# A hand-written order for TensorE: how long scan matmuls are held back for matmuls of the same array shape

## Chip, core and metric

The kernel runs on one core of a Trainium2 chip. The metric is the device time of one execution in microseconds (us). Before the change the median of three runs is 8417.75 us (8404.57 to 8426.19).

## What is computed

An image tensor `x` of shape (4, 96, 64, 64), so 4096 positions in each of 4 batches, goes through four residual layers:

```
x = x + L0(gn(x))        # 3x3 convolutions, a deformable convolution, and a selective scan in 4 directions
x = x + L1(gn(x))        # 3x3 convolution to 384 channels, gate, layer norm, 3x3 convolution back
t = tokens(x)
t = t + L2_attn(ln(t)); t = t + L2_ffn(ln(t))   # FFT over the 4096 tokens and back; a small quantized MLP
t = t + L3_attn(ln(t)); t = t + L3_ffn(ln(t))   # linear attention; the same kind of MLP
```

The part that sets the pace is the selective scan of L0, for 4 batches, 4 directions `k`, 192 channels and 16 states, over 4096 positions:

```
h = h * exp(dt * A) + (dt * u) * B      # per channel and state, position after position
y = sum over the 16 states of h * C
```

## The kernel before

**The scan.** It runs over batches, directions and four pieces of 1024 positions (`STEP`), 64 visits in all. One visit has 24 steps (`scan`, L1095 to L1179): 16 states for the first 128 channels, and 8 steps in which two states of the other 64 channels share the 128 partitions. So there are 64 x 24 = 1536 steps. Each does the following:

- SP loads one row of C, broadcast over the partitions (L1118 to L1126, tile `cb`, 3 buffers);
- PE broadcasts one row of B into the PSUM tile `pb` (L1127 to L1135, 2 buffers), with bf16 matmuls whose weights are 64x64 (four of them) or 64x128 (two of them);
- DVE multiplies `pb` by `dt*u` (L1136), ACT makes `hs = exp(dt*A)` (L1138, 5 buffers), DVE runs the scan over `hs` and `pb` (L1140), ACT copies the carry;
- POOL (in a few steps DVE) multiplies `hs` by `cb` (L1145);
- PE sums over the states by adding `hs` into the PSUM tile `yp` (L1146 to L1156), with f32 matmuls whose weights are 64x64 (four of them, `ident`) or 128x64 (two of them, `fold`).

**The fillers.** Everything else (the phases n, s, a, c, p, d and e: convolutions, norms, FFT, MLPs) is called the fillers here. Their matmuls are mostly of shape 128x128 in the array and write into only two PSUM tiles (`ps`, L600) as long as the scan runs. Once the scans are over, the tiles `pb` and one `yp` serve as further filler banks (L568 to L570).

**The order.** No scheduler of the framework orders the work. `Orders` records every operation, and `order()` (L303 to L492) plays the program through with estimated costs (`way`, `LATENCY`), always giving an engine the operation of the lowest rank among those whose inputs are ready at that time. The outcome is one fixed instruction stream for each engine, written out by `give()` (L498 and L504; so nearly every instruction in the profile has the line L504). A rank is the number of the scan step that the operation belongs to. `spread` (L1511) gives PE's fillers 300 added to their share of the steps (`LEAD`, L1577), so that a scan matmul goes ahead of nearly every filler that is ready too. The kernel's program is the same data flow whatever order comes out.

**The patience rule.** `part()` (L175) rounds the rows and columns of a matmul's weights up to 32, 64 or 128: this is its shape in the array. In the choice for PE (L387 to L396), the picked operation is put back if its shape differs from that of the matmul ordered last, no other ready operation has its shape, and fewer than `PATIENCE` nanoseconds have passed since its inputs were ready. The ready operation of the lowest rank that keeps the present shape goes first:

```
            if e == PE and ops[pick[1]].part != part and t < ops[pick[1]].ready + PATIENCE:
                if not any(ops[x[1]].part == ops[pick[1]].part for x in able[e]):
                    near = [x for x in able[e] if ops[x[1]].part == part]
```

The planner charges `CHANGE` = 95 ns for each change of shape.

**Zero matmuls.** Where PE would stand idle for more than 480 ns in the plan, and the columns streamed in the last 3413 ns are fewer than `WARM`, the planner inserts bf16 matmuls of zeros (L444 to L447, written out at L498; in the profile `yp<-nothing`). [...] `counted()` (L169) says how much a matmul counts for `WARM` and `ENOUGH`: its columns, four times for f32, in proportion to its rows, and by half for at most 64 weight columns.

**The end.** The fillers `phase_p`, `phase_d` and `phase_e` of the last batch need its scans, so they follow after them (L1563 to L1566), with more room and more banks.

Of the kernel before, what the change touches and what calls it, by code (L numbers as in the profile page):

```python
# [83 lines left out]

CHANGE = 95.0

PATIENCE = 1200.0

WARM, ZEROS = 8000, 512
PAGE = 2048  # L90
# [3 lines left out]
def columns(ap):  # L94
    n = 1
    for s in ap.shape[1:]:
        n *= s
    return n
# [6 lines left out]
class Orders:  # L105
# [63 lines left out]
    def counted(self, kwargs):  # L169

        k, m = kwargs["lhsT"].shape
        n = columns(kwargs["rhs"]) * (4 if kwargs["rhs"].dtype == F32 else 1)
        return n * k / 128 * (0.5 if m <= 64 else 1)

    def part(self, kwargs):  # L175

# [126 lines left out]
    def order(self):  # L303
# [58 lines left out]
        while ordered < len(ops):  # L362
# [15 lines left out]
            if e == ACT and ops[pick[1]].table not in (0, table):  # L378

                near = [x for x in able[e] if ops[x[1]].table in (0, table) and x[0] < pick[0] + 4]  # L380
                if near:
# [4 lines left out]
                    pick = other  # L386
            if e == PE and ops[pick[1]].part != part and t < ops[pick[1]].ready + PATIENCE:  # L387

# [1342 lines left out]
```

## Time and profile before

| | before |
|---|---|
| median of 3 runs | 8417.75 us |
| the profiled execution | 8409.08 us, its span 8407.3 us |
| first and last `pb` multiplication of the scan | 339.1 us and 7367.3 us after the start |
| matmul records on PE, zeros among them | 32888, 3672 |
| zero matmuls in the program | 3978 |
| mean granted TensorE clock | 0.95 |
| f32 matmul records, scan sums (`ident`) | 8192 for the program's 4096 |

Three things are needed to read it. First, an f32 matmul shows as two records in the profile, as the last row says. Second, matmuls overlap, so a record's own duration (some 0.6 us for 512 f32 columns) is not what it costs PE in a stream; the distance from one start to the next is. Third, "idle before, releaser" is the time that an engine stood idle in front of an instruction, with what ended it. Since each engine has a fixed stream, an instruction that isn't ready holds up everything behind it on its engine.

The profile falls into three stretches: a head until about 340 us without scans, the scans until about 7378 us, and a tail of 1029 us with fillers alone.

### The profile page before, as it was taken

To read this page: it belongs to the slowest core of one execution; us is meant where nothing else is said; L and a number is where in the kernel's file an instruction comes from. 1 tells how busy PE (TensorE), PEld (TensorE's weight loads), DVE (VectorE), ACT (ScalarE), POOL (GpSimd) and SP (SyncE) were. 2 spreads that over 40 slices of the span, in tenths; PEclk is the share of its full clock that TensorE was granted. 3 is DMA by queue.
4 is the path that set the end of the run, shared out by engine and by line. 5 is a ranking of instruction groups with operands and counts; after the bars stand their busy time and mean duration, and the time that the engine had idled before them with its cause. 6 is when DMAs were issued, how large, how long until landed. Compare 5 with 4: busy or idle time off the path is not lost. (4 is left out here: it accounts for less than half of the span.)

```text
span 8407.3 us, 101328 instructions
## 1 busy us (share of the span) xinstructions
PE 7487.2 (89%) x32888; PEld 2586.1 (31%) x33196; DVE 6557.9 (78%) x4658; ACT 4460.7 (53%) x7020; POOL 5317.5 (63%) x3147
## 2 busy tenths in 40 slices
PE   7898888989889998889989899978998899999989
PEld 2322222222222223232222222233322232244354
DVE  1398897777899999979898899986789999942324
ACT  3456644465646645555566666435465666423325
POOL 1278997865676668876776667685677667621202
PEclk8998999999999999999999999989999999999988
DMA  7688879899877788997678876889977866874442
GB/s 198 174 228 233 244 197 252 231 226 217 226 209 204 185 232 241 260 255 219 193 186 216 209 205 194 236 216 263 234 196 191 202 198 197 236 212 133 112 158 69
DMA packets 1247110, 1742.37 MB, mean 207 GB/s; under 512 B 607086, under 2 KB 683059, under 8 KB 1243636
## 3 DMA queue, kind: packets, MB, share of 16 engines
q1 hardware_dynamic: 1246580, 1735.87, 76.7%
q8 instruction: 263, 4.31, 0.2%
q14 instruction: 267, 2.19, 0.1%
HBM read 1473.58 MB, written 261.81 MB: 206 GB/s over the span
## 5 line engine op out<-in xcount | busy, mean ns | idle before, releaser
L504 POOL TENSOR_TENSOR arena<-arena 128x1024 f32<-128x1024 f32 (+3 forms) x2568 | 5012.4, 1974 | 2193.6 <-ACT arena L504 1150.7
L504 DVE TENSOR_TENSOR_SCAN arena<-arena,pb 128x1024 f32<-128x1024 f32 x1536 | 3573.7, 2329 | 288.3 <-ACT arena L504 173.7
L504 PE MATMUL ps<-arena 128*96 128x512 f32 (+10 forms) x8158 | 2774.4, 554 | 59.1 <-ACT arena L504 24.0
L504 ACT ACTIVATE arena<-arena,nega 128x1024 f32<-128x1024 f32 x1536 | 1754.8, 1149 | 1377.6 <-PE yp L504 1242.4
L504 DVE TENSOR_TENSOR pb<-pb,arena 128x1024 f32<-128x1024 f32 x1536 | 1860.7, 1213 | 338.6 <-PE pb L504 242.9
L504 PEld LDWEIGHTS ps<-arena 128*96 128x96 f32 (+6 forms) x8158 | 1028.5, 168 | 1463.7 <-issue 1219.8
L504 PE MATMUL yp<-arena,ident 64*64 64x512 f32 x8192 | 1137.7, 625 | 167.3 <-POOL arena L504 162.9
L498 PE MATMUL yp<-nothing 128*128 128x512 bf16 x3672 | 1005.0, 399 | 31.7 <-issue 24.4
L504 PE MATMUL pb<-arena,selb 64*64 64x512 bf16 x5120 | 626.8, 397 | 265.3 <-DVE arena L504 260.4
L504 PE MATMUL yp<-arena,fold 128*64 128x512 f32 x2048 | 579.4, 651 | 144.8 <-POOL arena L504 139.8
L504 ACT COPY arena<-arena 128x1 f32<-128x1 f32 x1536 | 283.4, 187 | 776.7 <-DVE arena L504 771.7
L504 ACT COPY arena<-ps 96x512 f32<-96x512 f32 (+6 forms) x636 | 332.8, 530 | 551.2 <-PE ps L504 494.2
L504 DVE TENSOR_TENSOR arena<-arena 96x512 f32<-96x512 f32 (+5 forms) x250 | 341.5, 1374 | 337.1 <-DMA arena<-rsd 135.9
L498 PEld LDWEIGHTS <-nothing 128*128 128x128 bf16 x3978 | 357.6, 101 | 767.0 <-issue 495.3
L504 ACT ACT_TABLE_LOAD x429 | 550.4, 1283 | 64.5 <-PE yp L504 53.5
L504 PEld LDWEIGHTS <-selb 64*64 64x64 bf16 x5120 | 202.0, 103 | 1089.1 <-issue 1084.1
L504 POOL TENSOR_TENSOR arena<-arena,half 128x4 f32<-128x4 f32 (+1 forms) x240 | 249.2, 1042 | 420.3 <-DMA arena<-vard 327.9
L504 PEld LDWEIGHTS yp<-arena,ident 64*64 64x64 f32 x8192 | 231.9, 133 | 793.2 <-POOL arena L504 405.1
L504 ACT CAST arena<-ps 128x512 bf16<-128x512 f32 (+2 forms) x542 | 305.4, 593 | 125.3 <-PE ps L504 117.3
L504 DVE BATCH_NORM_STATS2 arena<-arena 96x6 f32<-96x512 f32 (+1 forms) x192 | 130.4, 682 | 290.1 <-ACT arena L504 208.2
L504 PE MATMUL pb<-arena 64*128 64x192 f32 (+7 forms) x1104 | 304.3, 431 | 23.1 <-issue 9.6
L504 ACT ACTIVATE arena<-arena 96x512 f32<-96x512 f32 (+3 forms) x445 | 256.3, 591 | 116.3 <-DVE arena L504 109.5
(178 smaller groups left out, 4579.4 us busy)
## 6 DMA issues: line engine op xcount, KB each, us to landing
arena<-cr_d SPq DMA_DIRECT2D x1024, 512.0 KB
arena<-cr_d SPq DMA_DIRECT2D x1024, 256.0 KB
arena<-wmd SPq DMA_DIRECT2D x128, 576.0 KB
y_d<-arena SPq DMA_DIRECT2D x384, 128.0 KB
arena<-u_d SPq DMA_DIRECT2D x64, 512.0 KB
arena<-u_d SPq DMA_DIRECT2D x128, 256.0 KB
arena<-y_d SPq DMA_DIRECT2D x256, 128.0 KB
arena<-rsd SPq DMA_DIRECT2D x160, 192.0 KB
```

The costliest lines, as they stand in the source:

```text
L498: self.nc.tensor.matmul(i, start=alone, stop=alone, skip_group_check=True, **self.zeros)
L504: getattr(getattr(self.nc, NAMES[op.engine]), call)(*args, **kwargs)
```

## The change

`PATIENCE` goes from 1200 to 300, so a matmul that would change PE's array shape is held back for at most 300 ns of planned time. Besides, `counted()` counts a matmul with at most 32 weight columns as a quarter of its columns, where it was a half:

```diff
-PATIENCE = 1200.0
+PATIENCE = 300.0
...
-        return n * k / 128 * (0.5 if m <= 64 else 1)
+        return n * k / 128 * (0.25 if m <= 32 else 0.5 if m <= 64 else 1)
```

Nothing else is edited. The planner then writes out another order for every engine and, for the operations that may run on several engines, partly another engine.

## Prediction

> **What bounds the kernel now.** I read the page first, then three stretches, then who waited for whom, then DVE's largest groups, then a few microseconds of PE in order of time. Busy shares alone:
>
> ```profile
> PE 7487.2 (89%) x32888; PEld 2586.1 (31%) x33196; DVE 6557.9 (78%) x4658; ACT 4460.7 (53%) x7020; POOL 5317.5 (63%) x3147
> ```
>
> No engine is full over the whole span. Split at the first and last scan step (columns: span, then busy time and instructions of PE, PEld, DVE, ACT, POOL, granted clock, DMA share, GB/s):
>
> ```profile
> core 0: us, PE busy (x) PEld busy (x) DVE busy (x) ACT busy (x) POOL busy (x), PEclk, DMA share, GB/s
> 340.00:7378.00 7038.00, 6275.47 (x28280) 2020.51 (x28551) 6166.31 (x4001) 3968.40 (x6188) 5099.27 (x2893) 0.96 0.82 219
> 7378.00:8407.00 1029.00, 943.63 (x3607) 460.90 (x3630) 354.90 (x587) 363.14 (x624) 188.39 (x178) 0.93 0.47 137
> ```
>
> While scans run, DVE is 88% busy (6166 of 7038 us) and PE 89%, of which 841 us are zero matmuls (the same view for `nothing` alone). DVE idles 872 us. In the tail DVE is a third busy and PE 92%: the tail is PE's. The chain that ended last, complete only for the last 348 us, agrees: 25% of 1029 us, some 258 us of it, is PE. DVE's two scan instructions:
>
> ```profile
> L504 DVE TENSOR_TENSOR_SCAN arena<-arena,pb 128x1024 f32<-128x1024 f32 x1536 | 3573.7, 2329 | 288.3 <-ACT arena L504 173.7 <-DVE pb L504 4.1
> L504 DVE TENSOR_TENSOR pb<-pb,arena 128x1024 f32<-128x1024 f32 x1536 | 1860.7, 1213 | 338.6 <-PE pb L504 242.9 <-POOL arena L504 93.0 <-issue 1.2
> ```
>
> A step costs DVE 1213 + 2329 = 3542 ns, 1536 steps 5441 us: the floor of the scan stretch. PE makes DVE stall in two ways: directly, when the broadcast of B is late (243 us), and through ACT, whose exp needs an `hs` buffer that the sum over states has yet to read (part of 174 us). The waits, in us, times, longest:
>
> ```profile
> ACT arena L504 <- PE yp L504: 1345.6, 832, 11.2
> POOL arena L504 <- DMA arena<-cr_d: 610.2, 284, 8.0
> PE yp L504 <- POOL arena L504: 302.8, 270, 11.9
> PE pb L504 <- DVE arena L504: 270.2, 268, 10.7
> DVE pb L504 <- PE pb L504: 242.9, 199, 6.5
> ```
>
> So the coupling has two directions: DVE waits for PE 199 times, 1.22 us on average, and PE waits for DVE and POOL 573 us. And this is what a hold looks like (start, length, last the number of records):
>
> ```profile
> 2998.90 2.82 PE L504 MATMUL ps<-arena 128*96 128x512 f32 x6
> 3001.64 1.09 PE L504 MATMUL yp<-arena,ident 64*64 64x512 f32 x8
> 3002.67 0.39 PE L504 MATMUL pb<-arena,selb 64*128 64x512 bf16 x2
> 3002.89 1.02 PE L504 MATMUL ps<-arena 64*96 64x512 f32 x2
> 3003.84 1.09 PE L504 MATMUL yp<-arena,ident 64*64 64x512 f32 x8
> ```
>
> Runs of convolution matmuls stand between the scan's pieces. The weight loads of the run at 3005 us start every 0.43 us (3006.12, 3006.55, 3006.98), so a record costs 0.43 us and an f32 matmul, which is two, 0.86. Two records take 3003.84 - 3002.89 = 0.95 us up to the next shape, 0.09 more than 2 x 0.43. I take **0.09 us for a change of shape**.
>
> [...] PE stands 270 us before `pb` matmuls while fillers are queued behind them. [...] I use counts times distances for PE, not its 89%.
>
> **The change part by part.** The two programs' instruction orders can be compared without running; no time is in them, only counts.
>
> 1. *Shorter hold.* 300 ns is less than one 0.86 us filler, 1200 ns is up to two. A scan matmul that is ready while fillers of one shape run is let in about 0.9 us earlier. Taken stall by stall in the trace, with at most 0.9 us off each, DVE's waits for `pb` could lose 137 us and its waits for exp 70 us: **207 us** is the upper bound. Only stalls with a held choice gain; others come from a filler already running or from several sums in a row. The order gives a second measure. Before the last state sum stand 5550 filler matmuls now, and 5490 after the change; at the ends of batches 1, 2, 3 and 4 the lag is 72, 144, 78 and 60. Fillers go through at 5550/7378 us = 0.752 per us. If that rate stays, the scans end 60/0.752 = **80 us** earlier. I take 80, under half the bound; the other end is nothing, or a loss (rival 1).
>
> 2. *More changes of shape.* 4774 become 5132: 358 x 0.09 = 32 us of PE, 317 of them (29 us) before the last sum. They lie beside DVE's floor as long as PE has slack in zeros (841 us), and the 80 us contain them, since fillers squeezed by them lag. Without that cover they cost 29 us.
>
> 3. *Left-over fillers.* Sixty matmuls move past the scans into the tail: 34 convolutions, 6 centrings and 16 norm sums of 512 f32 columns (56 x 0.86 = 48 us) and 4 small ones. With 41 more changes (4 us) it is 52 us if PE is full there; by matmuls (60 of 1700 in 1029 us) it is 36. DVE's 23 more elementwise operations in the tail fall into its idle two thirds. I take **45**. The early tail is where they land, so they delay the last batch's own chain.
>
> 4. *The new count for narrow weights.* It lowers what single-column matmuls (norm sums) count for the clock, so it can only ask for more zeros. Yet zeros go from 3978 to 3957. At 3.34 us for 15 in the chain of waits, 0.22 each, that is 5 us less, in idle time anyway. I take 0; the bound is a few us each way.
>
> 5. *Other engines.* ACT's table loads go from 429 to 435, 6 x 1283 ns = 8 us, on an engine busy 53%: hidden. DVE takes over 7 wide products from POOL (7 x 2.4 = 17 us, from the 30 such groups it had) and gives up about as much else during the scans: 0. SP's queue of loads is reordered along with its readers; the order shows the same 7902 DMAs. A `cb` load that is behind another one now is in POOL's 610 us, and can become rival 2.
>
> The sum against the profiled execution's own 8409.08 us: -80 + 45 = -35, 8374. It is 8.7 us under the median of the runs, and the difference carries over: 8417.75 - 35 = **8383 us**.
>
> **Rivals.** (1) *PE's throughput is the limit, and it ends slower.* Then the scans end no earlier. PE's work over the whole program goes up by 32 us of changes less 5 us of zeros, so 8445; and because the stream is fixed, scan matmuls put earlier hold up the fillers behind them whenever DVE or POOL is later than planned: if PE's 573 us of such waits grow by a tenth, 8500. It decides as soon as the scans gain less than the 45 us that the tail costs. For it: PE's matmuls between two broadcasts, counted in the order at 0.86 us for 512 f32 columns, 0.22 for bf16, small shapes side by side once, 0.09 a change, come to 3.8 us on average with the zeros, more than DVE's 3.54; 60 left-over matmuls are hardly more than what the changes displace. Against it: 841 us of zeros are no work, and DVE does stall for `pb`. (2) *Another wait takes over.* DMA moves 219 GB/s at a share of 0.82 in the scans, and POOL waits 610 us for `cb`. If DVE's gain turns into waits of POOL for rows of C, the gain shrinks to about the tail's cost: 8418. For it: in some slices of the page DMA is at 9 tenths. Against: those waits are 284 of 1536 steps. (3) *All stalls in reach go*: -207 + 52 = -155, 8263. Against it: PE's longest runs between two broadcasts hardly get shorter in the order (238 stretches of over 5 us of PE's work become 220). (4) That the change does nothing is excluded: runs of 128x128 fillers rise from 1393 to 1611.
>
> **How the numbers follow.** Forecast (scans win 60 to 130 us, 8335 to 8392) 0.43; rival 3 and what lies towards it 0.13; rival 2 and small gains (8392 to 8443) 0.18; rival 1 0.26. About 0.3% (25 us) is what a measurement of this kernel can tell from no change. Faster is the first two, 0.56; within 0.3% 0.18; slower 0.26. The range leaves out a tenth on each side: from 8275, short of rival 3, to 8465, which takes in rival 1 without much blocking. The forecast's own range is 8335 to 8392.
>
> **What would show it.** Right: the last `pb` multiplication starts near 7290 us rather than 7367; DVE's wait for `pb` falls from 243 us towards 160; the tail grows from 1029 to about 1075. Wrong: the last multiplication comes no earlier (rival 1), PE's waits for DVE and POOL grow beyond 573 us (blocking), or POOL's wait for `cr_d` grows by as much as DVE's falls (rival 2). A tail that doesn't grow would make step 3 too dear.

## The result, and the profile after

The changed kernel takes 8480.94 us (median of four runs, 8462.86 to 8497.82); before stood at 8411.16 us beside it. The ratio is 1.0077, with a 95% interval of 1.0051 to 1.0103: slower, where 0.4% faster was forecast, and above the range. The profiled execution takes 8462.86 us, the fastest of the four and 53.8 us more than the one of before (8409.08 us). PE is TensorE, DVE VectorE, ACT ScalarE, POOL GpSimd, and SP SyncE, which issues the loads and stores.

First the stretches, split where the scans of this kernel begin and end (columns as before: span, busy time of PE, PEld, DVE, ACT, POOL, clock, DMA share, GB/s):

```profile
328.00:7353.00 7025.00, 6330.94 (x28408) 1978.30 (x28407) 6183.79 (x3996) 3962.33 (x6169) 5075.83 (x2869) 0.95 0.82 218
7353.00:8461.00 1108.00, 1021.46 (x3773) 481.18 (x3772) 365.22 (x610) 378.12 (x651) 192.54 (x182) 0.93 0.47 134
```

The scans are over a little earlier, but the tail has grown from 1029 to 1108 us, and PE is as full in it as before (92%, a tenth of the tail with zeros both times). The waits (total, times, longest):

```profile
ACT arena L504 <- PE yp L504: 1431.5, 893, 16.8
POOL arena L504 <- DMA arena<-cr_d: 613.2, 252, 11.9
PE yp L504 <- POOL arena L504: 259.3, 260, 8.2
PE pb L504 <- DVE arena L504: 213.6, 234, 6.1
DVE pb L504 <- PE pb L504: 176.8, 151, 7.2
```

DVE's wait for the broadcast of B fell from 242.9 to 176.8 us, as forecast. The two waits of PE for DVE and POOL did not grow but fell, from 573 to 473 us, and POOL's wait for rows of C stayed (610 and 613 us). DVE's two scan groups:

```profile
L504 DVE TENSOR_TENSOR_SCAN arena<-arena,pb 128x1024 f32<-128x1024 f32 x1536 | 3573.4, 2329 | 318.8 <-ACT arena L504 208.5 <-DVE pb L504 2.3
L504 DVE TENSOR_TENSOR pb<-pb,arena 128x1024 f32<-128x1024 f32 x1536 | 1859.8, 1212 | 274.4 <-PE pb L504 176.8 <-POOL arena L504 93.0 <-DMA arena<-f2p 1.9
```

The same work, 64 us less idle before the multiplication, but 30 us more before the scan (288.3 then): DVE's wait for ACT's exp, which was to shrink, grew from 173.7 to 208.5 us. And ACT waited longer for `yp`, 1431.5 us after 1345.6. So of what the earlier broadcasts saved, half was lost again at the exp. In the stretch of the scans DVE's idle time fell from 872 to 841 us, its work grew from 6166 to 6184 us, and the stretch begins 12 us earlier (328 after 340): -31 + 18 - 12 = -25 us at its end, and no more.

Where the time went is told by the last batch's fillers. The stores that end its phases, first in the kernel before, then after (the two starts are the first and the last of the kernel, and the last is the last batch's):

```profile
L504 SPq DMA_DIRECT2D x2p<-arena x32: 314/370/1321, 2242.4 to 7506.9; - x32
...
L504 SPq DMA_DIRECT2D x1d<-arena x32: 303/365/551, 2428.8 to 7616.8; - x32
...
L504 SPq DMA_DIRECT2D q_d<-arena x32: 303/319/1285, 3822.9 to 8338.1; - x32
```

```profile
L504 SPq DMA_DIRECT2D x2p<-arena x32: 303/368/709, 2335.3 to 7536.9; - x32
...
L504 SPq DMA_DIRECT2D x1d<-arena x32: 304/371/545, 2498.6 to 7657.1; - x32
...
L504 SPq DMA_DIRECT2D q_d<-arena x32: 303/320/574, 3990.1 to 8390.3; - x32
```

The last scan ends at 7371 us before and at 7347 after, 24 us earlier. Yet the first half of `phase_p` (`x2p`) ends 30 us later, its second half (`x1d`) 40, and the stores of queries 52. Counted from the last state sum, the first `x2p` row comes after 10 us before and after 68 us now. The same holds for the other batches: at their ends the scans stand 58, 40 and 51 us earlier than before, and the fillers' stores of `x2d` 97, 84 and 55 us later. The edit did give the scans PE's time, and the fillers, which end last, lost more than the scans won.

What stands at the head of the tail in the chain of waits of the changed kernel (start, length, what; some of its longest pieces):

```profile
7359.18 10.47 PE ps L504 x24
7371.54 12.36 PE pb L504 x28
7393.09 6.23 PE pb L504 x16
7415.71 4.94 POOL arena L504 x4
7421.53 4.79 DMA arena<-y_d
7430.32 5.50 DMA rsd<-arena
7436.80 4.75 DMA arena<-rsd
```

First some 30 us of left-over convolutions (until 7382 us), and only then the norm of the last `phase_p`, a chain of small DMAs. PE sums its first mean (weights `over`, 128*128) 34 us after the last state sum; in the kernel before this stood 39 us ahead of the last state sum.

### The profile page after: what moved, and what is told of

Read it like the earlier page. It is cut to its first block, busy times and chain, and to the rows that moved or that the text cites. A ratio compares the mean times of both kernels' runs of the same rounds, so it can differ in the third digit from the quotient of the medians.

```text
span 8461.1 us, 101588 instructions
## 1 busy us (share of the span) xinstructions
PE 7607.5 (90%) x33175; PEld 2559.4 (30%) x33175; DVE 6585.2 (78%) x4675; ACT 4468.6 (53%) x7029; POOL 5298.5 (63%) x3127
## 5 line engine op out<-in xcount | busy, mean ns | idle before, releaser
L504 DVE TENSOR_TENSOR_SCAN arena<-arena,pb 128x1024 f32<-128x1024 f32 x1536 | 3573.4, 2329 | 318.8 <-ACT arena L504 208.5
L504 DVE TENSOR_TENSOR pb<-pb,arena 128x1024 f32<-128x1024 f32 x1536 | 1859.8, 1212 | 274.4 <-PE pb L504 176.8
L504 PEld LDWEIGHTS ps<-arena 128*96 128x96 f32 (+7 forms) x8022 | 991.7, 168 | 1512.6 <-issue 1230.7
L498 PE MATMUL yp<-nothing 128*128 128x512 bf16 x3957 | 1069.0, 398 | 1.2 <-DVE half L504 1.2
L504 ACT ACT_TABLE_LOAD x435 | 558.1, 1283 | 76.4 <-PE yp L504 68.5
L504 PE MATMUL pb<-arena 64*128 64x192 f32 (+8 forms) x1080 | 302.7, 437 | 28.5 <-DMA arena<-f2p 9.1
L504 POOL MEMSET arena<- 96x16 f32 (+3 forms) x302 | 49.5, 179 | 427.6 <-PE ps L504 179.3
```

The lines of the kernel that those rows point to most:

```text
L498: self.nc.tensor.matmul(i, start=alone, stop=alone, skip_group_check=True, **self.zeros)
L504: getattr(getattr(self.nc, NAMES[op.engine]), call)(*args, **kwargs)
```

## The experiments

All times are ratios to the kernel before on the same chip. Theories: A, the fillers' use of PE ends the kernel, and changes of shape and interrupted runs cost it; B, the new count is the cause; C or L, it is the luck of the one order that came out.

**The change taken apart, a larger dose, and a neighbour.**

```diff
-PATIENCE = 1200.0
+PATIENCE = 300.0       # p300_alone
+PATIENCE = 2400.0      # p2400
+PATIENCE = 1190.0      # p1190_null
...
-        return n * k / 128 * (0.5 if m <= 64 else 1)
+        return n * k / 128 * (0.25 if m <= 32 else 0.5 if m <= 64 else 1)   # count_alone, PATIENCE 1200
```

> PATIENCE 300 with the old count of narrow weights. Theory A (more array-shape changes and interrupted fillers slow the chain of fillers that ends last): the order has 5100 changes against 4774, so the loss comes with it: +40 to +70 us, scans ending 20 to 60 us earlier and the tail longer by 60 or more. Rival B (the count is the cause): within 20 us of before. Rival C (which order comes out is luck): any time between -60 and +80, without a tie to the number of changes.

> PATIENCE 1200 with the new count. Its order has 4762 changes (12 fewer than before) and 4143 zero matmuls (165 more). Theory A: within 25 us of before. Rival B (the count is the cause): +40 to +70. Rival C (luck): anything from -60 to +80.

> PATIENCE 2400, the dose in the other direction, old count. 4539 changes (235 fewer), and 5684 fillers before the last sum (134 more). Theory A: faster, -20 to -60 us: scans end later than 7371 us, the tail is shorter than 1030 us by more. The forecast's own reasoning (late scan matmuls stall the vector engine): slower by 20 to 100, its wait for pb grows beyond 243 us. Rival C (luck): either.

> PATIENCE 1190, a change of under one percent of the wait: it changes some choice early on, after which the order differs everywhere, with 4760 changes against 4774. Theory A: within 15 us of before. Rival C (luck of the order): it shows the scatter that any other order brings; over 25 us either way would say that +54 to +70 us is not far outside it.

Measured: `p300_alone` 1.0004 (0.9993 to 1.0014), `count_alone` 1.0067 (1.0053 to 1.0081), `p2400` 1.0063 (1.0046 to 1.008), `p1190_null` 1.0041 (1.0027 to 1.0056). Theory A as put there missed all four: the shorter wait alone costs nothing here (its scans end at 7373 us, no earlier, and its tail is only 8 us longer), the count alone costs 56 us, the longer wait isn't faster, and 1190 isn't within 15 us. Rival B met the two runs that it spoke of, and the forecast's own reasoning met `p2400`: slower by 53 us, with a longer wait for `pb`. But a wait of 1190 instead of 1200, which means nothing, costs more than half of what the change costs. So one order for each setting can't tell a cause. At the far end of the dose, what moves is where the time lies. In `p2400`:

```profile
344.00:7506.00 7162.00, 6364.67 (x28968) 2072.26 (x28968) 6235.59 (x4032) 4021.67 (x6249) 5118.50 (x2913) 0.95 0.82 217
7506.00:8496.00 990.00, 893.78 (x3317) 431.29 (x3314) 314.77 (x537) 349.80 (x603) 169.59 (x159) 0.92 0.46 130
```

```profile
DVE pb L504 <- PE pb L504: 294.5, 182, 11.3
```

A longer wait gives the longest wait for `pb`, the latest scans and the shortest tail of all orders here: the reverse of the changed kernel.

**More neighbours, to see the scatter.** Only `PATIENCE` differs, with the old or the new count:

```diff
-PATIENCE = 1200.0
+PATIENCE = 1210.0      # p1210_null; with the new count c1210_null
+PATIENCE = 310.0       # p310_null; with the new count a310_null
+PATIENCE = 1190.0      # with the new count c1190_null
+PATIENCE = 290.0       # with the new count a290_null
```

> PATIENCE 1210, old count: a second neighbour of before, whose order differs from it as a matter of chance. If the order of before is a lucky one (theory L), slower by 0.2 to 0.7%, as PATIENCE 1190 was by 0.41%. If 1190 was the odd one, within 0.2%.

> PATIENCE 310, old count: a neighbour of PATIENCE 300 with the old count, which stood at 1.0004. Theory L (any other order costs 0 to 0.8%, patience does nothing on average): anywhere from 1.000 to 1.008. Theory P (a shorter wait helps by about 0.4% against neighbours of 1200): below 1.002 again.

> PATIENCE 310 with the new count: a neighbour of the changed kernel. Theory B (the new count costs some 0.6%, patience nothing): 1.006 to 1.009. Theory L (luck of the order): 1.000 to 1.008, where a time near 1.002 would show that the changed kernel's loss is no property of its two edits.

> PATIENCE 1190 with the new count: a neighbour of the run with the count alone, which stood at 1.0067. Theory B: 1.005 to 1.009. Theory L: 1.000 to 1.008. Its order has 4167 zero matmuls, 189 more than before; if zeros were what costs, it would be the slowest of the four.

> PATIENCE 1210 with the new count, a third neighbour of the run with the count alone (1.0067, 1.0044 so far). Theory B (the new count costs some 0.4% on average): 1.003 to 1.007. Theory L (only luck of the order, scatter 0.4%): anything from 0.995 to 1.008. It has 3896 zero matmuls, 82 fewer than before, where the two others had 165 and 189 more.

> PATIENCE 290 with the new count, a third neighbour of the changed kernel (1.0077, 1.0015 so far). Theory B: 1.003 to 1.008. Theory L: 0.995 to 1.008. Whatever the time, the shorter wait should show as before: the vector engine's wait for pb under 190 us, the scans done before 7371 us after the start, a tail over 1044 us.

Measured: `p1210_null` 0.9955 (0.9938 to 0.9972), `p310_null` 1.0035 (1.0024 to 1.0046), `a310_null` 1.0015 (1.0003 to 1.0028), `c1190_null` 1.0044 (1.0028 to 1.0061), `c1210_null` 1.0037 (1.0023 to 1.0051), `a290_null` 1.0005 (0.9993 to 1.0016). 1190 and 1210 lie 0.86% apart with before between them: theory L holds for any single setting, and `p1210_null` is faster than both kernels, where a lucky order of before would have had it slower. Theory P is out (1.0035), and theory B missed both neighbours of the changed kernel and `c1190_null` (1.0044, just below) and met `c1210_null`. The wait for `pb` of `a290_null` is 125 us and its tail 1065, as put there, but its scans end at 7378 us and not before 7371. Zero matmuls don't explain it: with the new count, 3896 of them (`c1210_null`) and 4167 (`c1190_null`) give nearly the same time.

**The price of a change of shape, with the order held.** Between two 128x128 matmuls that follow each other without a pause in the plan, at every fourth such place where a sum is open, one matmul of zeros with one column is added to the open sum; `extra_flat` adds it in the shape 128x128, so without a change:

```diff
+                if part == whole == op.part and opened is not None and t - free[PE] < 1:
+                    self.met += 1
+                    if self.met % 4 == 0:
+                        out.append((t, (opened, flip)))
...
+                self.nc.tensor.matmul(i[0][:64, :1], start=False, stop=False, skip_group_check=True, **self.one)
+    nc.one = {"lhsT": nothing[:64, :64], "rhs": nothing[:64, 128:129]}    # extra_flat: all 128 rows and columns
```

> The order of before, unaltered, with 765 added one-column matmuls of zeros of shape 64x64, each between two 128x128 matmuls that follow each other: 1530 more changes of shape, some four times the 358 of the change, and nothing else moves. Theory A (PE's time is what ends the kernel, a change costs 0.09 us): 1530 x 0.09 = 138 us and more, 1.016 or above. Slack theory (changes lie beside the vector engine's floor): under 40 us, below 1.005. A fourth of what is measured over the next run is what the change's own 358 cost.

> The same 765 added matmuls at the same places, of shape 128x128, so without any change of shape: the control. 765 x 0.03 to 0.1 = 25 to 75 us of PE if PE is the limit, within 20 us of before if there is slack.

Measured: 1.0171 (1.0155 to 1.0187) and 1.0050 (1.0033 to 1.0066). The added ones, and DVE's wait in the same kernel `extra_changes` (there the line that writes out the order is L513):

```profile
L503 PE MATMUL yp<-nothing x765: 187/188/212, 88.2 to 8570.6; 64*64 64x1 bf16 x192
```

```profile
DVE pb L513 <- PE pb L513: 270.3, 244, 5.2
```

One added matmul and the convolution behind it, in `extra_changes` and then in `extra_flat`:

```profile
3019.29 0.19 PE L503 MATMUL yp<-nothing 64*64 64x1 bf16 x1
3019.41 1.96 PE L513 MATMUL ps<-arena 128*96 128x512 f32 x4
```

```profile
3032.76 0.17 PE L503 MATMUL yp<-nothing 128*128 128x1 bf16 x1
3032.79 1.08 PE L513 MATMUL ps<-arena 128*96 128x512 f32 x2
```

Between two convolution records of this form (128*96, 512 columns) the distance from start to start is 430 ns in the median, 456 with the flat matmul between them and 639 with the other (159 places each). So a change of shape costs PE (639 - 456)/2 = 92 ns, as the forecast had it. At the end of the kernel, the difference of 1.21% of 8438 us (before beside them) is 102 us for 1530 changes, or 83 to 121 us by the two intervals: 0.067 us each, three quarters (0.6 to 0.9) of what they cost on PE. Taken together, added matmuls and changes cost PE 765 x 209 ns = 160 us, and 144 us (1.71%) arrive, nine tenths. DVE's wait for `pb` hardly moves (243 to 270 us) while the kernel grows by 143 us (medians), so DVE's floor hides little: by far the most of an added PE time reaches the end. Theory A is met, the slack theory is out. The change's 358 changes of shape thus cost some 24 us (19 to 28), 0.28%. Here the order is the same in all three kernels, and no luck is in it.

**Is it the count, or the order?**

```diff
-PATIENCE = 1200.0
+PATIENCE = 1180.0      # p1180_null
+PATIENCE = 1220.0      # p1220_null; with the new count c1220_null
+PATIENCE = 290.0       # p290_null
+PATIENCE = 320.0       # with the new count a320_null
+PATIENCE = 280.0       # with the new count a280_null
```

> PATIENCE 1180, old count. If the new count costs some 0.35% (theory B): 0.996 to 1.004, and below 1.002 on average with the next two. If there is only luck: 0.995 to 1.008, on average near 1.003.

> PATIENCE 1220, old count: the same two expectations as for 1180. It also tells whether 1210 at 0.9955 has a region of good orders about it (below 0.998) or stands alone.

> PATIENCE 290, old count: the same two expectations as for 1180. By the price of a change of shape alone (337 more than before, 0.067 us each: 23 us) 1.0027. The wait for pb under 190 us and a tail over 1044 us.

> PATIENCE 1220, new count: its order is the same as that of PATIENCE 1210 with the new count (1.0037) up to the third batch. Theory B: 1.002 to 1.007. Only luck: 0.995 to 1.008.

> PATIENCE 320 with the new count: a neighbour of the changed kernel, 298 more changes of shape than before. By the measured price of a change (0.067 us) alone 1.0024; with a cost of the new count of 0.4% on top 1.006; only luck 0.996 to 1.008. The vector engine's wait for pb under 190 us.

> PATIENCE 280 with the new count: a neighbour of the changed kernel, 361 more changes of shape than before. By the price of a change alone 1.0029; with the new count 1.007; only luck 0.996 to 1.008. The vector engine's wait for pb under 190 us.

Measured: `p1180_null` 0.9996 (0.9987 to 1.0004), `p1220_null` 1.0010 (1.0 to 1.0019), `p290_null` 1.0023 (1.0013 to 1.0033), `c1220_null` 1.0101 (1.0087 to 1.0115), `a320_null` 0.9973 (0.9963 to 0.9984), `a280_null` 1.0062 (1.0039 to 1.0086). In groups of neighbours (means; the last scan's end from the start, the tail from there, from one profile each):

| wait, count | kernels | ratio, mean and range | DVE's wait for `pb`, us | DVE's scans' wait for exp, us | last scan ends, us | tail, us |
|---|---|---|---|---|---|---|
| 1180 to 1220, old | 5 | 1.0000 (0.9955 to 1.0041) | 216 | 181 | 7404 | 1030 |
| 290 to 310, old | 3 | 1.0021 (1.0004 to 1.0035) | 167 | 205 | 7368 | 1082 |
| 1190 to 1220, new | 4 | 1.0062 (1.0037 to 1.0101) | 192 | 182 | 7453 | 1037 |
| 280 to 320, new | 5 | 1.0026 (0.9973 to 1.0077) | 154 | 214 | 7363 | 1080 |

The waits for `pb` are under 190 us in `p290_null`, `a320_null` and `a280_null`, as put there. The times fit no single theory: the three new orders with the old count average 1.0010, as theory B asks, but `c1220_null` lies above what either theory allows, and `a320_null` is faster than before, where B asks for 1.006. `c1210_null` and `c1220_null`, whose orders are the same up to the third batch, differ by 0.64%.

Three things stand out. On average the shorter wait takes a fifth to a quarter off DVE's wait for `pb`, adds 24 to 32 us to its wait for exp, ends the scans earlier and makes the tail 43 to 52 us longer, with either count. What it does to the time isn't told apart from the scatter: with the old count it costs 0.2% on average, about what the price of the shapes asks (0.28%), with the new count it gains 0.36%, and both are within two standard errors of nothing. And the changed kernel, at 1.0077, is the slowest of its five neighbours, whose mean is 1.0026: going by this mean, more than half of its loss (0.51 of 0.77%) belongs to the order that came out.

Whether the new count costs by itself stays open. Nine orders with it average 1.0042, eight without it 1.0008; with a scatter of 0.4% and 0.3% that is two standard errors. At waits of about 1200 the two groups hardly overlap, at about 300 they do.

**What the plan says of the order.** `order()` keeps the planned end of every operation and of the whole (`self.span`, L489); building a recorded kernel gives them without a chip. Before, the plan has the last scan end at 7016 us and the program at 8068; after the change, at 7007 and 8132. So the plan itself says that the scans win 9 us (24 measured) and the tail grows by 73 us (78 measured), and that the program gets longer by 0.79% (0.77% measured). Over `p2400` and the 17 kernels of the table, the planned tail, from the last scan on, is within 23 us of the profiled one, which goes from 990 to 1114 us, and the planned end of the program goes with the measured ratio at a correlation of 0.72. So much of what is called luck here, the tails above all, is written in the plan of the order that came out, and neighbouring settings get different plans.

## Why the prediction was wrong, point by point

- *What bounds the kernel.* "A step costs DVE 3542 ns ... the floor of the scan stretch" is true, and it isn't the limit. The scans were read as the pace, because DVE was 88% busy and stalled for PE. But they could finish 24 us earlier (7404 to 7363, 41 us, between the means of the first and last group) and the kernel still end later, since the work that follows them had grown. The 841 us of zeros, taken for PE's slack, weren't slack to count on: of the added changes of shape a quarter was hidden, of all added PE time a tenth.
- *Step 1, shorter hold.* This is the step that failed, in what it takes the scans to win. Its first way was right: 66 us less wait for `pb`, against the 137 that were in reach. Its second way went wrong: the wait for exp, where 70 us were in reach, grew by 35 us in this order and by 24 to 32 in the means of the groups. Why ACT gets its `hs` buffers later stays open. The failing term is "if that rate stays, the scans end 80 us earlier": they ended 24 us earlier. The fillers' rate did not stay: 5490 of them before the last sum, in 7353 us, are 0.747 per us, where 0.752 was taken, and this difference alone is some 55 us. A lag of fillers in the order was read as time won by the scans; it was for the greater part time lost by the fillers. "No time is in them, only counts" gave away the better source: the plan behind these orders has times, and they say 9 us.
- *Step 2, changes of shape.* 0.09 us was right as PE's own price (92 ns measured). "They lie beside DVE's floor" failed: where they were added alone, three quarters of it reached the end, which makes 24 us for the change.
- *Step 3, left-over fillers.* Right in kind, too small: 45 us against 78 in this order, though the means of the groups say 43 to 52. "They delay the last batch's own chain" was named and not priced: the norm of the last `phase_p` with its small DMAs starts only when the left-overs are through.
- The sum closes with these: -35 as forecast, +56 for scans that ended 24 us earlier instead of 80, +33 for the tail, make +54; the profiled executions differ by 53.8 us.
- *Step 4, the new count.* Wrong as argued. "It can only ask for more zeros" looked at `WARM` alone. Counted in the orders: with the new count in the test against `WARM` only, the order is that of before with 3 more zeros. With it only in the test against `ENOUGH`, where the planner doubles its own estimate of a matmul's cost after a window with few columns, the order is that of `count_alone`. So the edit changes the planner's estimates, and the whole order from the first batch on. That a matmul's cost on the chip follows this estimate was not shown here; the mean granted clock is 0.950 before and 0.948 after.
- *Step 5.* ACT's 435 table loads (1283 ns each) and POOL's waits for rows of C (613 us) are as forecast. DVE's zero isn't: its work in the scans grew by 18 us. Its wide products went from 30 to 37 (21 us) and five smaller ones left it (25 us), as forecast, but casts and products whose number stayed took 29 us longer; why stays open.
- *Rivals.* Rival 1, PE's throughput, came nearest: the scans gained less than the tail cost, as it asks. But its scans were to end no earlier, and they ended 24 us earlier; its 8445, from 32 us of changes less 5 of zeros, is 36 us short; and its second half (8500) is out, since PE's waits fell. Rivals 2 and 3 are out. No rival said that the outcome of a planner's reordering scatters by 0.3 to 0.4% whatever is meant by it. That is a gap of the forecast: the range was made from mechanisms alone, and they come to less than the scatter.

## What to carry to other kernels

If a planner writes the order, a change of one of its constants is one draw from a scatter: run some neighbours of the old and of the new setting before believing either. Read the times of the plan too, and not only the counts of the order: here they had the longer tail before any run. Work that runs beside the loop that stalls may still be what ends last, so ask in each stretch which chain finishes the kernel, and follow its stores from batch to batch in both traces. A cost on an engine with idle slots is measured by adding it alone, with the order held.

## What was not expected of the hardware

A change of the array's shape costs 0.09 us in a stream of matmuls, as taken, but of this 0.067 us (0.054 to 0.079) reach the end of a kernel in which PE is only 89% busy by the profile, at least 841 us of that with zeros during the scans (of 3978 zero matmuls the trace has kept 3672). A one-column matmul of zeros without a change of shape takes 0.026 us of PE between two convolution records (456 - 430 ns), and 765 of them cost the kernel 42 us (28 to 56), so 0.055 us each.
